# A ternary feed-forward kernel on one core: the second block, too, does layer 1 by seven products of halves

## The chip, the core and the metric

The kernel runs on one core of a Trainium2 chip. A core has five engines that work side by side, each through its own queue in order: TensorE (PE in the profile; its weight loads are PEld), VectorE (DVE), ScalarE (ACT), GpSimd (POOL) and SyncE (SP), which here only issues transfers. The metric is the time of one execution on the device in microseconds (us). For one execution there is also a trace of every instruction; its span is the time from the first instruction to the last.

## The reference

```python
w = weights[conditions]                          # one 64 x 64 matrix for each of 128 samples
c = jnp.einsum('bct,bcd->bdt', x, w)             # x: (128, 64, 512)
h = gelu(c @ ternary(W1).T + b1)                 # 512 -> 2048
y = h @ ternary(W2).T + b2                       # 2048 -> 512
# ternary(W) = alpha * sign(W) * (|W| > 0.05 * max|W|), alpha the mean of |W| where the mask holds
scale = jnp.max(jnp.abs(y)) / 7 + 1e-8           # over the whole of y
out = x + jnp.clip(jnp.round(y / scale), -7, 7) * scale
```

## The kernel before

The 128 samples make 8192 rows ("tokens") of 512 values. They are worked on in NB = 16 blocks of 512 tokens; a block is four pairs of samples. For each block the kernel does three things on TensorE: it mixes x by the samples' matrices (`mix`, into the PSUM tile `pc`), it does layer 1 (PSUM, then Gelu on ACT), and it does layer 2, which gathers in four PSUM tiles `py`. The 2048 hidden values are taken in NH = 16 steps of 128. Layer 2 runs LAG = 2 steps behind layer 1. The first is the exception: block 0 does all of its layer 1, then nearly all of its layer 2 (steps 0 to 13) in a loop of its own, in which ACT and DVE also finish preparing the weights.

To keep precision, every moving operand is held as two fp32r parts, hi and lo: ACT copies a tile to hi, DVE subtracts it to get lo (`split`), and each product is done with both. The ternary weights are kept as fp8 tiles `w1t` and `w2t`; before each use a step's weights are widened into fp32r (`widen1`, `widen2` on POOL; `widen7` on POOL and, for group 2, on DVE).

There are two forms of a block.

- An ordinary block (`eight`): each step is 8 matmuls of 512 columns for layer 1 and 8 for layer 2. Its x is conditioned by `condition`: four pairs j, for each a mix on PE, one ACT copy to hi and one DVE subtraction to lo, in a pair of large tiles `x`.
- A block in SEVEN (`pair`, `seven`): two steps at a time. Layer 1 of the two is a 2 x 2 product of halves, done with seven products in place of eight, each of 4 matmuls of 256 columns, into the PSUM tiles `xy` and `z`. It needs sums of quarters of x (`t1` to `t4`) and sums of quarters of the weights (`w1f[1]` to `w1f[3]`), and DVE and ACT put the products together in `ring`. Its x is conditioned by `condition7`: for each pair j a mix, three ACT copies out of `pc` (`b12`, the hi parts of `xb` and `xl`), four DVE sums over x in place, two DVE subtractions (lo of `xb` and `xl`), and then a part that is returned to the caller, one ACT copy of the four sums to hi (`xt`) and one DVE subtraction to lo. In `pair` that last part runs in the following pair of steps; in `eight` it runs at once:

```python
for part in condition7(n + 1, j, extra["x"][:, j % 2, :], two_next[-1]):
    part()
```

Everything is issued through `InOrder`, which pins an instruction behind all that was written before it for the same engine. So the text of the program is the order of each engine's queue. In the loop of block 0's layer 2 this order is, after the matmuls of step hc:

```python
if hc in (4, 6, 8, 9):        # g = 0, 1, 2, 3
    count2(g)                 # ACT: masks <- terns, with a sum
    kept(w2t, g, terns2)      # ACT: the fp8 weights of layer 2
if hc in (5, 7, 9, 11):       # j = 0, 1, 2, 3
    condition(1, j, pair_of(x_next, j), two_next)
    for g in {7: [0], 9: [1], 11: [2, 3]}.get(hc, []):
        sum2(g)               # DVE: nat <- nat, terns, with a sum
```

Ahead of these, at steps 0 and 3, DVE has `signed2(2)` and `signed2(3)` (`terns` from `nat` and `junk`), and at step 1 six subtractions `low`. `alpha_2` turns the sums of `count2` and `sum2` into the scale of layer 2 (a small matmul `total`, then four small DVE instructions); the first `result` (DVE: y out of `py`) needs it. PSUM holds two `pc` tiles at a time, two of `ph` (or `xy`) and four of `py`; in the blocks of SEVEN `z` takes one of the two places of `pc`.

SyncE's queue issues all loads of x and the stores. POOL's queue also gathers the samples' matrices (`fetch`) and puts them in place (`place`).

Of the kernel before, what the change touches and what calls it, by code (L numbers as in the profile page):

```python
# [19 lines left out]
P = 128  # L20
# [17 lines left out]
def tile_cond_ternary_ffn(  # L38
# [24 lines left out]
    GH = NH // NG  # L63
    WCH = GH * T
    LAG = 2
    SEVEN = range(2, 14)
    KNOWN = NB - 2
    AWAY = 2
    HALF = BLK // 2
# [172 lines left out]
    def flat(w):  # L242
        return w.rearrange("p a b -> p (a b)")
# [10 lines left out]
    def group1(tiles, g):  # L254
        return tiles[g // 2][:, g % 2, :]
# [118 lines left out]
    def widen2(n, hc):  # L374
        if n == 0 and hc < NH - LAG:
            w = w2f[hc % 4]
        elif n == NB - 1 and hc == NH - 1:

            w = flat(w1f[0])
        else:  # L380
            w = w2f[hc % 2]
        if n == 0 and hc < NH - LAG:
            g, i = divmod(hc, GH)
            pool.tensor_copy(w, group1(terns2, g)[:, i * T : (i + 1) * T])
        else:
            pool.tensor_copy(w, w2t[:, hc])
        wide2[n, hc] = w
# [28 lines left out]
    def low(n, hc):  # L416

        open_low.pop((n, hc), lambda: None)()
# [202 lines left out]
    w1t = big.tile([P, NH, T], F8, tag="big", name="w1t")  # L621
    x_next = load_x(1)

    def kept(t, g, tiles):

        act.copy(flat(t[:, g * GH : (g + 1) * GH]), group1(tiles, g), saturate=False)

    for hc in range(NH - LAG):
        if hc + 2 < NH - LAG:
            widen2(0, hc + 2)  # L630
        layer2(0, hc)
        if hc == 0:
            signed2(2)
        if hc == 1:
            for i in range(10, NH):
                low(0, i)
        if hc < NG:
            kept(w1t, hc, terns)
        if hc == 3:
            signed2(3)  # L640
        if hc == 4:
            two_next = parts(1)
            w2t = big.tile([P, NH, T], F8, tag="big", name="w2t")
        if hc in (4, 6, 8, 9):
            g = {4: 0, 6: 1, 8: 2, 9: 3}[hc]
            count2(g)
            kept(w2t, g, terns2)
        if hc in (5, 7, 9, 11):
            j = (hc - 5) // 2
            condition(1, j, pair_of(x_next, j), two_next)  # L650
            for g in {7: [0], 9: [1], 11: [2, 3]}.get(hc, []):
                sum2(g)
    cond[1] = two_next
    x_next, two_next, fetched = [], [], []
    hf = ring[:2]
    widen1(1, 0)
    widen2(0, NH - LAG)

    w1p = w1t.rearrange("p (k two) m -> p k two m", two=2)
    a11, a12 = w1p[:, :, 0, : 2 * P], w1p[:, :, 0, 2 * P :]
    a21, a22 = w1p[:, :, 1, : 2 * P], w1p[:, :, 1, 2 * P :]
# [51 lines left out]
    def quarter_x(n, j):  # L716

        sp.dma_start(out=extra["x"][:, j % 2, :], in_=x_blk[n][:, j, :])

    def product(out, w, b, first):  # L720
        for c in range(2):
# [149 lines left out]
    def eight(s):  # L871

        n, hc = steps[s]
        if s + 1 < len(steps):
            ahead = steps[s + 1]
            if ahead[0] not in SEVEN:
                widen1(*ahead)
            else:
                for g in (3, 0):
                    widen7(0, g)  # L880
        widen2(*steps[s + 1 - LAG])
        if n + 1 < NB:
            if hc == 0:
                if n + 1 == SEVEN[0]:
                    extra["x"] = half.tile([P, 2, T], F32, tag="half", name="x_quarters")
                    for j in range(2):
                        quarter_x(n + 1, j)
                else:
                    x_next.append(load_x(n + 1) if n + 1 < NB - 1 else split_x(n + 1))
                two_next.append(parts7(n + 1) if n + 1 in SEVEN else parts(n + 1))  # L890
            if 2 <= hc < 2 + PAIRS:
                fetched.append(fetch(n + 1, hc - 2))
            if 7 <= hc < 7 + PAIRS:
                place(hc - 7, fetched[hc - 7 - PAIRS])
        if n == KNOWN and hc in (0, 1):
            fetch_x(order[hc])
        two = half.tile([P, 2, BLK], F32R, tag="half", name=f"h_{n}_{hc}")
        two = [two[:, k, :] for k in range(2)]

        for part in halves if s == len(steps) - 1 else [slice(0, BLK)]:  # L900
            ph = ps_h.tile([P, BLK], F32, tag="ph", name=f"ph_{n}_{hc}_{part.start}")
            ph = ph[:, part]
            layer1(n, hc, ph, part)

            bend(n, hc, ph, [t[:, part] for t in two], ph if n == NB - 1 else hf[hc % 2])
        hidden[n, hc] = two
        if s + 1 < len(steps) and steps[s + 1][0] in SEVEN and n not in SEVEN:
            widen7(0, 1)
            widen7(0, 2)
        if n + 1 < NB and 8 <= hc < 8 + PAIRS:  # L910
            j = hc - 8
            if n + 1 in SEVEN:
                for part in condition7(n + 1, j, extra["x"][:, j % 2, :], two_next[-1]):
                    part()
                if j + 2 < PAIRS:
                    quarter_x(n + 1, j + 2)
            else:
                condition(n + 1, j, pair_of(x_next[-1], j), two_next[-1])
            cond[n + 1] = two_next[-1]
        if hc == LAG:  # L920
            for j in range(PAIRS):
                largest(n - 1, j)
            keep(n - 1)
        if n == KNOWN and hc == LAG:
            tops_known.append(widened(ymax[:, :KNOWN], "known"))
        if s == len(steps) - 1:
            return
        if s == NH + 1:
            alpha_2()
        layer2(*steps[s - LAG])  # L930
        if steps[s - LAG][1] == NH - 1:
            for j in range(PAIRS):
                result(n - 1, j)
        if n == KNOWN and hc == LAG + 1:
            largest_of(tops_known.pop(), top_known, ps_c, "pc")
            steps_of(scale, inverse, top_known)
        if n == KNOWN and hc > LAG + 1:
            advance(2 if hc in (6, 9, 12, 15) else 1)
        if n == NB - 1:
            advance(1)  # L940
# [15 lines left out]
    def pair(n, k, finish):  # L956

        s = n * NH + 2 * k
        ahead = (k + 1) % (NH // 2)
        leaves = ahead == 0 and n + 1 not in SEVEN  # L960
        before = steps[s - 2], steps[s - 1]

        def second(i):
            layer2(*before[i // PAIRS], [i % PAIRS])

        def results(js):
            for j in js:
                result(n - 1, j)

        def behind(i):  # L970
            if i == 0:
                finish()
                if k == 1:
                    results(range(2, PAIRS))
                widen2(*before[1])
                if k == 0:
                    two_next.append(parts7(n + 1) if n + 1 in SEVEN else parts(n + 1))
            if i == 1 and not leaves:
                widen7(ahead, 1)
            if i == 2:  # L980
                if parting:
                    parting[0][0]()
                if leaves:
                    widen1(n + 1, 0)
                else:
                    widen7(ahead, 0)
            if i == 4:
                if not leaves:
                    widen7(ahead, 3)
                if k < PAIRS:  # L990
                    fetched.append(fetch(n + 1, k))
                if 2 <= k < 2 + PAIRS:
                    place(k - 2, fetched[PAIRS * (n - 1) + k - 2])
                if not leaves:
                    widen7(ahead, 2)
                if parting:
                    parting.pop()[1]()
                if k == 1:
                    quarter_x(n + 1, 0)
                    quarter_x(n + 1, 1)  # L1000
                if k in (4, 5):
                    quarter_x(n + 1, k - 2)
                if 3 <= k < 3 + PAIRS:
                    xp = extra["x"][:, (k - 3) % 2, :]
                    if n + 1 in SEVEN:
                        parting.append(condition7(n + 1, k - 3, xp, two_next[-1]))
                    else:
                        condition(n + 1, k - 3, xp, two_next[-1])
                    cond[n + 1] = two_next[-1]
            if i == 5:  # L1010
                widen2(*steps[s])
            if i == 6 and k == 0:
                results([0])
            if i == 7:
                if k == 0:
                    results([1])
                if k in (1, 2):
                    for j in (2 * k - 2, 2 * k - 1):
                        largest(n - 1, j)
                if k == 2:  # L1020
                    keep(n - 1)

        return seven(n, k, behind, second)
# [131 lines left out]
```

## Time and profile before

| What | Value |
|---|---|
| Median of 3 runs | 999.9 us (999.79 to 1000.32) |
| The profiled execution | 999.93 us |
| Its span | 998.1 us |
| Mean granted TensorE clock in it | 0.996 |
| PE busy | 983.1 us (98%) |
| DVE, ACT, POOL busy | 693.1 (69%), 603.1 (60%), 577.0 us (58%) |
| Share of PE in the chain that ended last | 97% |

The page of the profile gives the busy time of each engine and the chain of work that ended last, followed back from the last instruction. The views in order of time list an engine's instructions, neighbours of one kind merged: start, length, engine, line, operation, output and inputs with their shapes, count, and in brackets the idle time before it and who ended it. Nearly all instructions bear line 34, that of the helper `InOrder`; they are told apart by their tiles. Numbers of tiles are left out: `wf` is `w1f` and `w2f`, `x` the tiles of `condition`, `h` the hidden parts, `nat`, `terns`, `masks` and `junk` those of the weights' preparation.

### The profile page before, as it was taken

Reading aid. Unit: us, or ns where it says so; the run is one execution under the profiler, and the core shown is the slowest. Engines: PE = TensorE matmul, PEld = TensorE weight load, DVE = VectorE, ACT = ScalarE, POOL = GpSimd, SP = SyncE. Lnnn points to the kernel's source line nnn. Section 1 sums busy time; section 2 is a strip of 40 time slices with the busy share of each in tenths; the row PEclk is TensorE's granted clock in tenths of the full one; section 3 lists DMA queues with packets and bytes.
Section 4 is the critical chain, followed back from the end, with each engine's and each line's share of the span. In section 5 each row is a group of like instructions: output and inputs, shape, how many; then the busy total and the mean of one; then the engine's idle time right before and its main releaser. Section 6 shows DMA issues by size and latency. Waiting matters only on the chain.

```text
span 998.1 us, 17056 instructions
## 1 busy us (share of the span) xinstructions
PE 983.1 (98%) x5865; PEld 869.1 (87%) x5866; DVE 693.1 (69%) x1316; ACT 603.1 (60%) x1078; POOL 577.0 (58%) x916
## 2 busy tenths in 40 slices
PE   8999999999999999999999999999999999999995
PEld 5887889999999998999999999999999989888884
DVE  7897347677677767677677676767667675567865
ACT  7994445656556565565655565565565655467663
POOL 6866446566564655656565564655656556465433
PEclk9999999999999999999999999999999999999998
DMA  9201011110111101011110011101011110349993
GB/s 360 85 22 45 15 32 49 32 56 20 28 47 34 57 23 68 14 32 48 34 56 24 24 47 41 50 23 66 14 33 48 33 58 23 128 157 367 384 408 121
DMA packets 33159, 80.06 MB, mean 80 GB/s; under 512 B 3760, under 2 KB 3760, under 8 KB 30128
## 3 DMA queue, kind: packets, MB, share of 16 engines
q1 hardware_dynamic: 31024, 76.86, 21.6%
q0 software_dynamic: 2048, 2.10, 0.7%
q8 instruction: 47, 0.77, 0.3%
q14 instruction: 40, 0.33, 0.1%
HBM read 46.44 MB, written 32.51 MB: 79 GB/s over the span
## 4 chain that ended last, share of the span: by engine, by line
PE 97%; DVE 2%; DMA 1%; ACT 0%; SPq 0%; issue 0%
PE py L34 46%; PE xy L34 18%; PE z L34 14%; PE ph L34 12%; PE pc L34 6%; DMA nat<-in_L_ffn_W 1%; DVE top L34 1%; DVE xt L34 0%; PE number L34 0%; DVE ymax L34 0%; DVE y_last L34 0%; SPq L34 0%; DVE x L34 0%; ACT x L34 0%; ACT ph L34 0%
## 5 line engine op out<-in xcount | busy, mean ns | idle before, releaser
L34 PE MATMUL py<-wf,h 128*128 128x512 f32 x2048 | 498.4, 394 | 0.0
L34 PEld LDWEIGHTS py<-wf,h 128*128 128x128 f32 x2048 | 376.5, 188 | 76.5 <-DVE y L34 1.6
L34 POOL CAST wf<-w2t 128x512 fp32r<-128x512 fp8e4 x242 | 167.1, 696 | 219.1 <-PE py L34 215.1
L34 DVE TENSOR_TENSOR ring<-xy,ring 128x256 f32<-128x256 f32 x192 | 107.0, 557 | 171.7 <-PE xy L34 169.1
L34 DVE TENSOR_TENSOR h<-ring,h 128x512 fp32r<-128x512 f32 x236 | 173.0, 757 | 73.9 <-ACT h L34 73.7
L34 ACT ACTIVATE ring<-ring,b1t,alpha_w 128x512 f32<-128x512 f32 x192 | 152.3, 817 | 84.3 <-DVE ring L34 84.3
L34 POOL CAST wf<-w1t 128x256 fp32r<-128x256 fp8e4 (+1 forms) x240 | 131.4, 550 | 69.9 <-PE xy L34 37.6
L34 ACT COPY ring<-xy 128x256 f32<-128x256 f32 x192 | 72.1, 375 | 150.9 <-PE xy L34 150.9
L34 POOL TENSOR_TENSOR wf<-w1t 128x256 fp32r<-128x256 fp8e4 x192 | 126.4, 658 | 51.8 <-PE xy L34 29.0
L34 ACT CAST h<-ring 128x512 fp32r<-128x512 f32 x240 | 142.3, 618 | 1.7
L34 PE MATMUL ph<-x,wf 128*128 128x512 f32 (+1 forms) x528 | 125.8, 384 | 0.3 <-DVE x L34 0.3
L34 PE MATMUL xy<-xt,wf 128*128 128x256 f32 x768 | 123.5, 283 | 0.0
L34 PE MATMUL xy<-xb,wf 128*128 128x256 f32 x768 | 122.7, 282 | 0.0
L34 PEld LDWEIGHTS xy<-xb,wf 128*128 128x128 f32 x768 | 111.7, 190 | 7.5
L34 PEld LDWEIGHTS ph<-x,wf 128*128 128x128 f32 x528 | 96.6, 188 | 20.1 <-DVE x L34 0.5
L34 PE MATMUL z<-xt,wf 128*128 128x256 f32 x768 | 107.8, 283 | 0.0
L34 PEld LDWEIGHTS xy<-xt,wf 128*128 128x128 f32 x768 | 106.0, 192 | 0.0
L34 PEld LDWEIGHTS z<-xt,wf 128*128 128x128 f32 x768 | 99.1, 192 | 0.0
L34 ACT COPY ring<-z 128x512 f32<-128x512 f32 x96 | 56.4, 587 | 56.4 <-PE z L34 56.4
L34 POOL COPY diag<-wg 64x64 f32<-64x64 f32 x128 | 48.7, 380 | 44.6 <-DMA wg<-in_L_cond_weights,rows 42.1
L34 ACT ACTIVATE ring<-ph,b1t,alpha_w 128x512 f32<-128x512 f32 x48 | 37.3, 778 | 57.4 <-PE ph L34 57.0
L34 POOL DMA_INDIRECT wg<-in_L_cond_weights,rows x64 | 64.0, 1000 | 11.6 <-issue 3.7
(111 smaller groups left out, 973.2 us busy)
## 6 DMA issues: line engine op xcount, KB each, us to landing
xt<-in_x SPq DMA_DIRECT2D x38, 512.0 KB, 7.5
y_dram<-y SPq DMA_DIRECT2D x15, 1024.0 KB, 3.9
out<-xt SPq DMA_DIRECT2D x30, 512.0 KB, 7.3
x_quarters<-in_x SPq DMA_DIRECT2D x52, 256.0 KB, 2.6
nat<-in_L_ffn_W SPq DMA_DIRECT2D x6, 1024.0 KB, 13.6
y_back<-y_dram SPq DMA_DIRECT2D x2, 1024.0 KB, 10.7
nat<-in_L_ffn_W SPq DMA_DIRECT2D x3, 512.0 KB, 9.6
wg<-in_L_cond_weights,rows POOLq DMA_INDIRECT x64, 2.7
```

The source lines that it names most:

```text
L34: return lambda *args, **kw: self._tc.keep_in_program_order(make(*args, **kw))
```

## The change

SEVEN begins with block 1 in place of block 2. Block 1's x is therefore conditioned by `condition7`, in the loop of block 0's layer 2, on x as it was loaded in one piece, with the last part run at once. At the end of that loop the first pair's weights are made by `widen7` for groups 3, 0, 1 and 2 in place of one `widen1`. The first block of `eight` after block 0 is now block 14, so `eight` loses its passage into SEVEN, and the quarters of x for block 2 are issued from `pair`. `alpha_2` moves from the second step of block 1 to a place behind the layer 2 of block 1's first pair. In the new text the functions of the seven products stand ahead of the loop, with nothing in them changed.

```diff
-    SEVEN = range(2, 14)
+    SEVEN = range(1, 14)
...
     for hc in range(NH - LAG):
...
         if hc == 4:
-            two_next = parts(1)
+            two_next = parts7(1)
             w2t = big.tile([P, NH, T], F8, tag="big", name="w2t")
...
         if hc in (5, 7, 9, 11):
             j = (hc - 5) // 2
-            condition(1, j, pair_of(x_next, j), two_next)
+            for part in condition7(1, j, pair_of(x_next, j), two_next):
+                part()
             for g in {7: [0], 9: [1], 11: [2, 3]}.get(hc, []):
                 sum2(g)
...
-    widen1(1, 0)
     widen2(0, NH - LAG)
+    for g in (3, 0, 1, 2):
+        widen7(0, g)
+    extra["x"] = half.tile([P, 2, T], F32, tag="half", name="x_quarters")
...
# in eight
-            if ahead[0] not in SEVEN:
-                widen1(*ahead)
-            else:
-                for g in (3, 0):
-                    widen7(0, g)
+            widen1(*ahead)
...
-                if n + 1 == SEVEN[0]:
-                    extra["x"] = half.tile([P, 2, T], F32, tag="half", name="x_quarters")
-                    for j in range(2):
-                        quarter_x(n + 1, j)
-                else:
-                    x_next.append(load_x(n + 1) if n + 1 < NB - 1 else split_x(n + 1))
-                two_next.append(parts7(n + 1) if n + 1 in SEVEN else parts(n + 1))
+                x_next.append(load_x(n + 1) if n + 1 < NB - 1 else split_x(n + 1))
+                two_next.append(parts(n + 1))
...
-        if s + 1 < len(steps) and steps[s + 1][0] in SEVEN and n not in SEVEN:
-            widen7(0, 1)
-            widen7(0, 2)
...
-        if s == NH + 1:
-            alpha_2()
         layer2(*steps[s - LAG])
...
# in pair, behind(i)
             if i == 6 and k == 0:
+                if n == 1:
+                    alpha_2()
                 results([0])
```

More of the change, by code (lines that the diff above doesn't have):

```diff
@@ L622, in tile_cond_ternary_ffn @@
     x_next = load_x(1)
[L624 to L641, printed above, removed]
-            two_next = parts(1)
[L643 to L649, printed above, removed]
-            condition(1, j, pair_of(x_next, j), two_next)
[L651 to L655, printed above, removed]
-    widen1(1, 0)
-    widen2(0, NH - LAG)
     w1p = w1t.rearrange("p (k two) m -> p k two m", two=2)
@@ L718, in quarter_x, with kept @@
         sp.dma_start(out=extra["x"][:, j % 2, :], in_=x_blk[n][:, j, :])
+    def kept(t, g, tiles):
+        act.copy(flat(t[:, g * GH : (g + 1) * GH]), group1(tiles, g), saturate=False)
+    for hc in range(NH - LAG):
+        if hc + 2 < NH - LAG:
+            widen2(0, hc + 2)
+        layer2(0, hc)
+        if hc == 0:
+            signed2(2)
+        if hc == 1:
+            for i in range(10, NH):
+                low(0, i)
+        if hc < NG:
+            kept(w1t, hc, terns)
+        if hc == 3:
+            signed2(3)
+        if hc == 4:
+            two_next = parts7(1)
+            w2t = big.tile([P, NH, T], F8, tag="big", name="w2t")
+        if hc in (4, 6, 8, 9):
+            g = {4: 0, 6: 1, 8: 2, 9: 3}[hc]
+            count2(g)
+            kept(w2t, g, terns2)
+        if hc in (5, 7, 9, 11):
+            j = (hc - 5) // 2
+            for part in condition7(1, j, pair_of(x_next, j), two_next):
+                part()
+            for g in {7: [0], 9: [1], 11: [2, 3]}.get(hc, []):
+                sum2(g)
+    cond[1] = two_next
+    x_next, two_next, fetched = [], [], []
+    hf = ring[:2]
+    widen2(0, NH - LAG)
+    for g in (3, 0, 1, 2):
+        widen7(0, g)
+    extra["x"] = half.tile([P, 2, T], F32, tag="half", name="x_quarters")
     def product(out, w, b, first):
@@ L906, in eight @@
         hidden[n, hc] = two
-        if s + 1 < len(steps) and steps[s + 1][0] in SEVEN and n not in SEVEN:
-            widen7(0, 1)
-            widen7(0, 2)
         if n + 1 < NB and 8 <= hc < 8 + PAIRS:
             j = hc - 8
[L912 to L918, printed above, removed]
+            condition(n + 1, j, pair_of(x_next[-1], j), two_next[-1])
             cond[n + 1] = two_next[-1]
```

## The prediction

> **What bounds the kernel now.** I read the page first (busy shares, then the chain that ended last), then PE in order of time, then ACT and DVE beside it in the stretch that the change rewrites.
>
> ```profile
> PE 983.1 (98%) x5865; PEld 869.1 (87%) x5866; DVE 693.1 (69%) x1316; ACT 603.1 (60%) x1078; POOL 577.0 (58%) x916
> ...
> PE 97%; DVE 2%; DMA 1%; ACT 0%; SPq 0%; issue 0%
> ```
>
> TensorE is busy 98% and carries 97% of the chain: a matmul column saved is time saved, as long as PE's operands are there. PE around block 1 (start, length, instruction):
>
> ```profile
> 82.60 1.98 PE L34 MATMUL ph<-x,wf 128*128 128x512 f32 x8
> ...
> 145.30 0.64 PE L34 MATMUL xy<-xb,wf 128*128 128x256 f32 x4
> ...
> 146.75 0.71 PE L34 MATMUL xy<-xt,wf 128*128 128x256 f32 x4
> ...
> 152.39 0.64 PE L34 MATMUL xy<-xb,wf 128*128 128x256 f32 x4
> ...
> 205.12 0.64 PE L34 MATMUL xy<-xb,wf 128*128 128x256 f32 x4
> ```
>
> Block 1 (ordinary) runs from 82.60 to 145.30, 62.70 us. Block 2 (seven products) from 145.30 to 205.12, 59.82 us; its first pair takes 7.09, the other seven 52.73. The third product of a pair, the first that needs w1f[2], starts 1.45 after the pair.
>
> Now ACT and then DVE during block 0's layer 2, where block 1's x is conditioned:
>
> ```profile
> 66.03 0.58 ACT L34 CAST x<-pc 128x512 fp32r<-128x512 f32 x1
> 66.51 1.91 ACT L34 ACTIVATE masks<-terns 128x2048 bf16<-128x2048 bf16 x1
> ...
> 68.41 1.89 ACT L34 CAST w2t<-terns 128x2048 fp8e4<-128x2048 bf16 x1
> ```
>
> ```profile
> 69.48 2.58 DVE L34 SCALAR_TENSOR_TENSOR terns<-nat,delta_w,junk 128x2048 bf16<-128x2048 f32 x1
> 71.98 1.27 DVE L34 TENSOR_TENSOR x<-pc,x 128x512 fp32r<-128x512 f32 x2
> 73.18 2.28 DVE L34 CUSTOM_DVE_ANT_0 nat<-nat,terns 128x2048 f32<-128x2048 f32 x1
> ...
> 78.69 0.69 DVE L34 TENSOR_TENSOR x<-pc,x 128x512 fp32r<-128x512 f32 x1 [3.22 <-ACT x L34]
> ```
>
> ACT runs without a gap here; a count2 and a kept together take 3.69 (66.51 to 70.20, where the next copy of x starts). DVE is 6 us behind: ACT has made hi of pair 0 at 66.03, DVE comes to its lo at 71.98. Today this doubles as slack, since each ACT copy needs only PE, and DVE follows at leisure. What the seven-product conditioning does when its last copy is not put off is seen in block 1, where block 2's x is made this way (ACT, then DVE):
>
> ```profile
> 116.02 0.26 ACT L34 COPY x_quarters<-pc 128x128 f32<-128x128 f32 x1
> ...
> 116.44 0.28 ACT L34 CAST xl<-pc 128x128 fp32r<-128x128 f32 x1
> 117.79 0.62 ACT L34 CAST xt<-x_quarters 128x512 fp32r<-128x512 f32 x1 [1.08 <-DVE x_quarters L34]
> ```
>
> ```profile
> 116.75 0.28 DVE L34 TENSOR_TENSOR x_quarters<-x_quarters,pc 128x128 f32<-128x128 f32 x1
> 116.95 0.81 DVE L34 TENSOR_TENSOR x_quarters<-pc,x_quarters 128x128 f32<-128x128 f32 x3
> ...
> 118.45 0.69 DVE L34 TENSOR_TENSOR xt<-x_quarters,xt 128x512 fp32r<-128x512 f32 x1 [0.16 <-ACT xt L34]
> ```
>
> ACT makes three copies (0.70 from the first start to the last end), then waits in its queue until DVE has made four sums (1.01), then copies hi; DVE's lo waits for that. It is a there-and-back between two queues, and the change puts it four times into the stretch where they are full.
>
> **The change part by part.** *Products.* A pair of ordinary steps has 16 layer-1 matmuls of 512 columns, 8 in 1.81 us by PE's rows, so 3.62. Seven products take 3.35 (152.39 to layer 2 at 155.74). Eight pairs: 2.2 us less. [...] Block against block the gain is 62.70 - 59.82 = 2.9, since block 1 also has a stop of 0.6 for y at 92 and the 0.14 of `total`.
>
> *The conditioning, walked through both queues.* DVE gets free for pair 0 at 71.98, as now: four sums to 72.99, then hi on ACT at 73.02. ACT, whose copies of pair 0 ended at 66.7, has stood 6.3 us, and everything behind hi in its queue (three count2 and kept, three pairs) is late. It goes on at 73.55, does count2(1) and kept(1) to 77.24, the copies of pair 1 to 77.94. DVE (lo of pair 0 done, 74.3) waits for these, 3.6 us; its sums end 78.98, hi(1) on ACT is 79.01 to 79.54 (to the next start), lo(1) ends 80.28, sum2(0) at 2.20 (79.30 to 81.50 in the trace) 82.48. ACT now has two count2 and two kept: 79.54 + 7.38 = 86.92; copies of pair 2 to 87.62; DVE has waited another 5.2. Sums to 88.66, hi(2) to 89.22, lo(2) to 89.96, sum2(1) to 92.16. ACT's copies of pair 3 are done at 89.92, but DVE's sums for it come after sum2(1): 92.16 to 93.17, its xb lo at 93.5, hi(3) to 93.8, lo(3) to 94.47. Then sum2(2) and sum2(3), 4.40: 98.87. Only then does DVE come to `widen7(0, 2)`, which now stands behind all this: first w1f[2] (0.42) at 99.29.
>
> *PE.* The 3rd mix needs pc of pair 0 back, 73.5, on time. The 4th needs that of pair 1 back, 79.5 instead of 78.07, so steps 12 and 13 end at 84.0 instead of 82.5. Then PE is out of work: product b11 needs xb of all pairs (93.5), the products with t1 and t4 need lo(3) (94.6), the one with t2 needs w1f[2] (99.32). That last wait ends latest: the pair stands as if begun at 99.32 - 1.45 = 97.87. Pair 1 follows at 104.96, block 2 at 104.96 + 52.73 = 157.69 against 145.30: **+12.4**, with the products' gain in it.
>
> *POOL and SP.* widen2(0, 14) waits for kept(3), now 86.9 instead of 78.1, and behind it stand widen7 of groups 3, 0 and 1 (0.64, 0.62, 0.64 + 0.40): done by 90, before 93.5, they cost nothing under that wait; without it 2.9 us of POOL work would stand against the 1.8 of step 13, about 1 us. The four gathers for block 2 (1.0 us each) move from steps 2 to 5 to pairs 0 to 3, the place that all later blocks use. The first two quarters of x, issued at 56.64, now go out in pair 1 and land in 2.6 us, needed in pair 3: nothing.
>
> *alpha_2.* Its matmul now stands behind the pair's layer 2, so DVE's first result of block 0 starts after it: 0.15 after pair 1's start plus 0.83 (90.33 to 91.16), where block 2 has it at 1.16 before (151.23). Two us late, and DVE has no idle time there: from 151.23 to 155.09 it goes straight into pair 1's additions. These come 2.1 late; gelu, casts and lo shift as far, and in pair 2 the copy of z must wait for the lo of hidden step 3, which reads the same ring tile: product t2 0.55 late, p5 1.06 late, and 0.25 for y in pair 1. With `total` 0.14: **+2.0**. Bounds: 0.14 if slack takes it, 2.2 if all of the delay lands.
>
> *The clock.* No stretch of the trace has PE idle for long; the record says 1.00 throughout. Its only cold stretch is the start, counted in 512-column matmuls:
>
> ```profile
> 3.00:7.00 4.00, 4.00 (x10) 1.38 (x10) 1.73 (x5) 0.88 (x1) 2.15 (x3) 1.00 0.96 395
> 7.00:15.00 8.00, 8.00 (x37) 3.55 (x36) 7.76 (x7) 7.49 (x5) 2.87 (x7) 1.00 1.03 393
> ```
>
> (PE's are the first count.) Ten in 4 us, then 37 in 8: 8.5 are missing at 0.216, 1.8 us. [...] Here PE is idle some 9 us, then 4 more ahead of t2. By the trace alone (1.00 throughout) the sum would have nothing[...]. I take **+1.8**, the cold row.
>
> Sum: 12.4 + 2.0 + 1.8 = 16.2 on the profiled execution's 999.93 us (span 998.1 and 1.8 around it), which stands 0.03 above the median of 999.9: **1016.1**.
>
> **The rivals.** *It works as meant.* If block 0's layer 2 covered the conditioning, block 1 would cost what block 2 does: 2.9 less, 997. For it: PE is the bound, and after 83 ACT is mostly idle. It decides in faster's favour only if w1f[2] is ready by 82.6 + 1.45 + 2.9 = 87.0; my walk misses that by 12, before alpha_2 and the clock. Against: DVE alone has 75.5 to 78.69 free, and gets 4 x 1.45 + 0.9 = 6.7 us more.
>
> *Only the work counts, not the order.* If ACT did not stand in hi (its later copies passing it), DVE would run on: today's end of sum2 at 87.31, plus 6.7, less the 3.2 idle: 90.8, so t2 at about 90.4 and pair 1 at 96.1. That is 8.9 less than the main case, near 1007. Against: 117.79 shows ACT standing for DVE with work behind it.
>
> *Worse.* The seven-product tiles take one more large buffer; if w2t got the one that `junk` leaves at 72.06, kept(0) would stand until then, the first sums come at 74.6 instead of 71.98, and all shifts by 2.6: 1018.7. [...]
>
> **How the numbers follow.** Main case 0.75, order free 0.10, worse 0.08, as meant 0.05, and 0.02 that the parts cancel to within 0.2% (2 us, about what a measurement of this kernel can tell from no change). Bounds of the main case: 16.2 - 1.8 - 1.86 = 12.5 to 16.2 + 1.6 + 0.2 = 18. I take 2 us below for some forty hand-overs added by hand, and above the buffer's 2.6: 1010.4 to 1020.4; left out are the order-free and the as-meant case. Faster 0.05, same 0.02, slower 0.93.
>
> **What would show it.** ACT waiting for DVE about 6.3 us ahead of its first `xt` cast at 73; DVE waiting for ACT 3.6 and 5.2 us before 88; a hole in PE from about 84 to 93.5 and one to 99.3 ended by DVE `wf`; a granted clock under 1.00 there; block 2's first `xy` near 161.5. I am wrong if PE's hole is under 5 us, if hi does not stand for DVE, or if something other than DVE's queue ends the hole.

## The result: 17 us slower, and the profile after

The changed kernel takes 1017.08 us (median; 1016.72 to 1018.11), the kernel before 1000.03 beside it: a ratio of 1.0173 (95% interval 1.0161 to 1.0184). Predicted were 1016.1, with a range of 1010.4 to 1020.4. The profiled execution took 1017.08 us, its span is 1015.3.

The busy shares and the chain that ended last, of the changed kernel:

```profile
PE 985.1 (97%) x5961; PEld 874.8 (86%) x5962; DVE 715.9 (71%) x1380; ACT 614.7 (61%) x1114; POOL 583.2 (57%) x932
...
PE 91%; DVE 5%; ACT 2%; issue 1%; DMA 1%; SPq 0%; ACTq 0%; DVEq 0%
```

PE has 96 more matmuls (8 pairs, 28 of 256 columns in place of 16 of 512). It has fewer columns and is busy 2.0 longer; part of its work ran at a lower clock, as seen below. DVE has 22.8 us more to do, ACT 11.6. The chain is the line to look at: PE carried 97% of it before and 91% now, and what it lost went to DVE and ACT. PE in order of time shows where (start, length, instruction, and in brackets the idle time before it and who ended it):

```profile
90.27 0.55 PE L34 MATMUL xy<-xb,wf 128*128 128x256 f32 x1 [5.46 <-ACT xb L34]
94.14 1.01 PE L34 MATMUL xy<-xb,wf 128*128 128x256 f32 x3 [3.33 <-DVE xb L34]
...
100.04 1.19 PE L34 MATMUL xy<-xt,wf 128*128 128x256 f32 x4 [2.99 <-DVE wf L34]
...
107.19 0.72 PE L34 MATMUL xy<-xb,wf 128*128 128x256 f32 x4
...
110.16 0.74 PE L34 MATMUL xy<-xt,wf 128*128 128x256 f32 x4 [1.31 <-ACT ring L34]
...
111.64 0.74 PE L34 MATMUL z<-xl,wf 128*128 128x256 f32 x4 [0.26 <-ACT ring L34]
...
116.35 0.64 PE L34 MATMUL xy<-xb,wf 128*128 128x256 f32 x4
...
162.07 0.64 PE L34 MATMUL xy<-xb,wf 128*128 128x256 f32 x4
```

PE has done block 0's layer 2 at 84.8 and then stands three times: for a hi and a lo of x, and for the weights w1f[2]. The second pair starts at 107.19 and takes 9.16 to the third at 116.35, where block 2's takes 7.01. From there block 1 runs as block 2 does: 45.72 for six pairs. Block 2 starts at 162.07 in place of 145.30, 16.77 later, nearly all of the 17.

Who stood for whom before that, ACT first and then DVE, in order of time:

```profile
73.39 0.63 ACT L34 CAST xt<-xt 128x512 fp32r<-128x512 f32 x1 [6.35 <-DVE xt L34]
```

```profile
78.34 0.29 DVE L34 TENSOR_TENSOR xt<-xt,pc 128x128 f32<-128x128 f32 x1 [3.60 <-ACT xl L34]
...
88.02 0.29 DVE L34 TENSOR_TENSOR xt<-xt,pc 128x128 f32<-128x128 f32 x1 [5.08 <-ACT xl L34]
...
99.48 0.42 DVE L34 TENSOR_TENSOR wf<-wf,w1t 128x256 fp32r<-128x256 f32 x1
```

ACT waits for DVE first, because hi needs DVE's sums; then DVE waits twice for ACT, which had been kept from its weights by the first wait. Neither engine was short of work in its queue. The last line is w1f[2], ready at 99.90: PE's third wait.

The stretches of PE's holes (span, then busy time and instructions of PE, PEld, DVE, ACT, POOL, then the granted clock, the DMA share and GB/s):

```profile
84.00:93.00 9.00, 1.36 (x5) 0.63 (x3) 4.79 (x11) 5.21 (x10) 5.49 (x6) 0.80 0.00 0
...
101.00:103.00 2.00, 2.00 (x12) 2.00 (x11) 0.42 (x1) 0.37 (x1) 0.81 (x2) 0.50 0.00 0
103.00:105.00 2.00, 2.00 (x12) 1.69 (x12) 1.83 (x4) 1.49 (x2) 1.24 (x2) 0.98 0.00 0
```

The granted clock is 0.50 from 89.43 to 103.08 (windows of half a microsecond give these ends). What PE does from 100.04 on, it does at half speed for 3 us: from one start to the next, four matmuls take 0.86 from 101.03, and 0.48 from 118.26.

### The profile page after: what moved, and what is told of

Its sections match the earlier page's. It is cut to its first block, busy times and chain, and to the rows that moved or that the text cites. A ratio compares the mean times of both kernels' runs of the same rounds, so it can differ in the third digit from the quotient of the medians.

```text
span 1015.3 us, 17395 instructions
## 1 busy us (share of the span) xinstructions
PE 985.1 (97%) x5961; PEld 874.8 (86%) x5962; DVE 715.9 (71%) x1380; ACT 614.7 (61%) x1114; POOL 583.2 (57%) x932
## 4 chain that ended last, share of the span: by engine, by line
PE 91%; DVE 5%; ACT 2%; issue 1%; DMA 1%; SPq 0%; ACTq 0%; DVEq 0%
PE py L34 43%; PE xy L34 20%; PE z L34 15%; PE ph L34 8%; PE pc L34 5%; DVE h L34 1%; DVE xt L34 1%; DMA nat<-in_L_ffn_W 1%; DVE nat L34 1%; DVE top L34 1%; ACT masks L34 1%; DVE junk L34 1%; ACT w2t L34 1%; DVE terns L34 1%; PE number L34 0%
## 5 line engine op out<-in xcount | busy, mean ns | idle before, releaser
L34 ACT ACTIVATE ring<-ring,b1t,alpha_w 128x512 f32<-128x512 f32 x208 | 165.1, 817 | 92.2 <-DVE ring L34 92.2
L34 POOL TENSOR_TENSOR wf<-w1t 128x256 fp32r<-128x256 fp8e4 x208 | 136.4, 656 | 66.1 <-PE xy L34 34.3
L34 PE MATMUL xy<-xb,wf 128*128 128x256 f32 x832 | 134.4, 284 | 8.8 <-ACT xb L34 5.5
L34 PE MATMUL xy<-xt,wf 128*128 128x256 f32 x832 | 134.5, 284 | 4.3 <-DVE wf L34 3.0
L34 PEld LDWEIGHTS xy<-xb,wf 128*128 128x128 f32 x832 | 121.7, 192 | 17.4 <-POOL wf L34 5.9
L34 PEld LDWEIGHTS xy<-xt,wf 128*128 128x128 f32 x832 | 115.4, 193 | 4.8 <-issue 3.3
L34 PE MATMUL z<-xt,wf 128*128 128x256 f32 x832 | 117.8, 284 | 0.0
L34 PE MATMUL ph<-x,wf 128*128 128x512 f32 (+1 forms) x400 | 94.2, 383 | 0.3 <-DVE x L34 0.3
L34 PEld LDWEIGHTS ph<-x,wf 128*128 128x128 f32 x400 | 72.6, 188 | 15.1 <-DVE x L34 0.5
L34 POOL DMA_INDIRECT wg<-in_L_cond_weights,rows x64 | 64.4, 1006 | 11.6 <-issue 3.6
L34 PE MATMUL z<-xl,wf 128*128 128x256 f32 x416 | 67.5, 285 | 0.3 <-ACT ring L34 0.3
```

Source lines behind the costliest of these rows:

```text
L34: return lambda *args, **kw: self._tc.keep_in_program_order(make(*args, **kw))
```

## The experiments

Each time is the median of its kernel; the kernel before, run beside them, stood at 1000.01 to 1000.04. All start from the changed kernel unless another is named.

**The order of hi.** Is it that ACT's copy to hi stands for DVE's sums with work queued behind it? The parts of the conditioning that come last (hi, lo) are put off by two steps or more for pairs 0 to 2:

```diff
-            for part in condition7(1, j, pair_of(x_next, j), two_next):
-                part()
+            if hc in (9, 11):
+                for _ in range(len(put_off) if hc == 9 else 1):
+                    for part in put_off.pop(0):
+                        part()
+            put_off.append(condition7(1, j, pair_of(x_next, j), two_next))
+            if hc == 11:
+                for part in put_off.pop(0):
+                    part()
```

> Only the place of the put-off part of the conditioning changes: ACT's copy of the four sums to hi and DVE's lo of pairs 0 and 1 come at step 9 behind the last kept, that of pair 2 at step 11 ahead of pair 3's copies. Same instructions, same count. Theory (ACT standing in hi for DVE, with count2 and kept behind it, is what stretches both queues): ACT has its last kept done at about 78.7 instead of 87.3, DVE its last lo at 87.1 and w1f[2] at 92.0; the product with t2 starts near 92 instead of 100.0, so about 8 us less, and up to 1.3 less again if the clock does not fall: 1007.5 to 1009. Rival (the added DVE work itself is what is too much, in whatever order): under 2 us gained, 1015 or more.

Measured: 1010.28 (1009.28 to 1010.72), ratio to before 1.0099 (1.0083 to 1.0114). PE in order of time:

```profile
86.00 0.38 PE L34 MATMUL xy<-xb,wf 128*128 128x256 f32 x1 [2.67 <-POOL wf L34]
...
92.89 1.20 PE L34 MATMUL xy<-xt,wf 128*128 128x256 f32 x4 [2.98 <-DVE wf L34]
```

With the same instructions in another order the product with w1f[2] comes at 92.89 in place of 100.04. That is 7.15, and 6.8 of it arrives in the time. The order is the largest cause, as the theory had it; the time lies 1.3 above its band. The clock fell here too (0.50 from 87.05 to 97.3), which the expectation had left open: 3.55 from this product to the layer 2. When it fell, only stops of 2.67 and 0.40 lay behind PE; the one of 2.98 came later.

**What stands ahead of w1f[2] on DVE.** The last two sums go behind `widen7`:

```diff
-            for g in {7: [0], 9: [1], 11: [2, 3]}.get(hc, []):
+            for g in {7: [0], 9: [1]}.get(hc, []):
                 sum2(g)
...
         widen7(0, g)
+    sum2(2)
+    sum2(3)
```

> Only DVE's order changes: the first pair's weights of group 2 come ahead of sum2 of groups 2 and 3 instead of behind them. Theory (the end of PE's hole is set by w1f[2] standing behind two sums of 2.2 us): the product with t2 follows the products with t1 and t4 at about 97 instead of 100.0, 3 us less, 1014.0; the two sums then delay the pair's additions and alpha_2, but these wait for PE anyway. Rival (the hole is set by the conditioning's lo, and the sums only change places with the additions): within 0.5 us of 1017.1, since what w1f[2] gains is given back at the results.

Measured: 1014.26 (1013.0 to 1014.95), ratio 1.014 (1.0125 to 1.0156). The same product starts at 96.73, with no wait, and the second pair at 103.98 in place of 107.19. The third of PE's waits was DVE's order alone, and it cost about 3.

**alpha_2.** It goes back ahead of the layer 2 of the pair:

```diff
# in pair, behind(i)
+                if n == 1 and k == 0:
+                    alpha_2()
...
-                if n == 1:
-                    alpha_2()
                 results([0])
```

> Only the place of alpha_2 changes: its matmul stands ahead of the layer 2 of block 1's first pair instead of behind it. Theory (the second pair's 9.16 us against 7.01 come from DVE's results starting 2 us late, behind alpha_2): the second pair takes about 7.0, the whole 2.0 to 2.2 less, 1015.0. Rival (the second pair is slow from the backlog of DVE out of block 0 or from the cold clock): within 0.3 us of 1017.1.

Measured: 1015.19 (1014.92 to 1015.86), ratio 1.0149 (1.0134 to 1.0165). PE in order of time:

```profile
108.11 0.64 PE L34 MATMUL xy<-xb,wf 128*128 128x256 f32 x4
...
115.12 0.64 PE L34 MATMUL xy<-xb,wf 128*128 128x256 f32 x4
```

The second pair takes 7.01 again, 2.15 less than in the changed kernel. In this execution the clock stayed low for 17.1 us (0.50 from 88.2 to 105.3) and the first pair's layer 2 lay partly in that spell: 4.47 in place of 3.66, which took back about 0.8.

**The clock.** PE's first hole is filled with 44 idle matmuls of tiles that lie there (128x512, bf16, 212 ns each), with no other edit:

```diff
+    warm = ps_h.tile([P, T], F32, tag="ph", name="warm")
+    for _ in range(44):
+        pe.matmul(out=warm, lhsT=ones_b, rhs=group2(3)[:, :T], start=True, stop=True)
```

> 44 matmuls of 512 bf16 columns into a PSUM tile that nobody reads are added behind step 13's layer 2, to fill PE's hole from 84.8 to about 94; everything else is as after the change. Theory (the clock fell to half from 89.4 to 103.05 because PE was idle, and this made the first pair's products 1.34 us longer): the granted clock stays 1.00, 1.3 to 1.4 less, 1015.7. Rival (the products were slow for another reason, operands for one, or the clock falls for another cause): the clock stays up and the time stays within 0.3 us of 1017.1. If the 44 take longer than the hole, some of the gain is given back.

Measured: 1017.51 (1016.73 to 1017.76), ratio 1.0172 (1.0158 to 1.0186): no gain, and neither theory's reason. The matmuls held the clock at 1.00 through the first hole. PE and the windows behind the second:

```profile
100.08 0.80 PE L34 MATMUL xy<-xt,wf 128*128 128x256 f32 x4 [3.76 <-DVE wf L34]
```

```profile
100.00:101.00 1.00, 0.92 (x6) 0.95 (x7) 0.39 (x1) 0.09 (x1) 0.92 (x2) 0.78 0.00 0
101.00:102.00 1.00, 1.00 (x7) 1.00 (x7) 0.16 (x1) 0.28 (x1) 0.43 (x2) 0.50 0.07 16
...
104.00:105.00 1.00, 1.00 (x6) 0.78 (x5) 0.93 (x3) 0.80 (x2) 0.85 (x2) 1.00 0.00 0
```

The second hole, 3.76 us, was enough by itself. The clock fell at about 100.6, half a microsecond after PE had begun to work again, and the work then ran at half speed for 3.4 us. So both holes are filled, the second by 16 more behind the first products of the pair:

```diff
+            if i == 1 and n == 1 and k == 0:
+                again = ps_c.tile([P, T], F32, tag="pc", name="warm_again")
+                for _ in range(16):
+                    pe.matmul(out=again, lhsT=ones_b, rhs=group2(3)[:, :T], start=True, stop=True)
```

> As the run that filled PE's first hole, with 16 further idle matmuls between the pair's products with t4 and t2, so that both holes are filled (3.4 of the 3.75 us of the second). There the clock held through the first hole and fell for 3.4 us just after the second. Theory (each hole[...] costs the clock, and the clock is worth 1.3 us here): the granted clock stays 1.00 through the pair, the products from t2 to layer 2 take 2.0 us instead of 3.3, and the time is 1.3 less than after the change, 1015.8. Rival (the clock is not what makes this pair slow, or filling matmuls cost as much as they save): within 0.4 us of 1017.1.

Measured: 1015.47 (1015.28 to 1017.16), ratio 1.0157 (1.0143 to 1.0171), 1.6 below the changed kernel's median, though the two intervals overlap. The place itself is plainer. In PE's order:

```profile
100.26 0.71 PE L34 MATMUL xy<-xt,wf 128*128 128x256 f32 x4 [0.29 <-DVE wf L34]
...
102.25 3.82 PE L34 MATMUL py<-wf,h 128*128 128x512 f32 x16
```

The clock is 1.00 in every window from 93 to 109, and the product with w1f[2] is 1.99 ahead of the layer 2, as in block 2; in the changed kernel it was 3.33. The clock costs 1.34.

**All of the order at once.** The last parts of the conditioning go where DVE has had time, `widen7` stands ahead of the sums, `kept(3)` stands last, the sums of groups 0 and 1 go behind the loop, and those of groups 2 and 3 wait for the first pair:

```diff
-        if hc in (4, 6, 8, 9):
+        if hc in (4, 6, 8):
...
+        if hc == 8:
+            put_off.pop(0)()
+            put_off.pop(0)()
         if hc in (5, 7, 9, 11):
-            for part in condition7(1, j, pair_of(x_next, j), two_next):
-                part()
-            for g in {7: [0], 9: [1], 11: [2, 3]}.get(hc, []):
-                sum2(g)
+            hi, lo = condition7(1, j, pair_of(x_next, j), two_next)
+            put_off.append(lambda hi=hi, lo=lo: (hi(), lo()))
+        if hc == 9:
+            count2(3)
+        if hc == 10:
+            for g in (3, 0, 1, 2):
+                widen7(0, g)
+            put_off.pop(0)()
+        if hc == 11:
+            put_off.pop(0)()
+            kept(w2t, 3, terns2)
...
-    for g in (3, 0, 1, 2):
-        widen7(0, g)
+    sum2(0)
+    sum2(1)
...
# in pair, behind(4), n == 1 and k == 0
+                    sum2(2)
+                    sum2(3)
```

> The same instructions as after the change in another order. ACT: count2 and kept of groups 0 to 2, then hi of pairs 0 and 1, pair 2's copies, count2(3), hi of pair 2, pair 3's copies and hi, and kept(3) last. DVE: the first pair's weights of group 2 ahead of lo of pair 2, and no sum2 in the loop: groups 0 and 1 behind it, 2 and 3 behind the first pair's additions. Theory (order made the hole): lo of pair 3 is done at 82.3 and PE finds its operands at 82.9, no hole and no fall of the clock. What is left is DVE's amount of work: its sums end near 93.4, alpha_2 is 3.5 us late for the second pair's layer 2, and with the delay this hands to the third pair the time is 1001 to 1003. Rival (order cannot cure it, DVE and ACT have too much to do ahead of block 1): a hole of over 5 us stays, 1006 or more.

Measured: 1004.88 (1004.84 to 1005.45), ratio 1.0049 (1.0035 to 1.0063): 12.2 less than the changed kernel, 1.9 above the expected band, and still slower than before. PE:

```profile
82.80 0.64 PE L34 MATMUL xy<-xb,wf 128*128 128x256 f32 x4
...
94.78 0.36 PE L34 MATMUL total<-sums,ones_f 128*128 128x8 f32 x2 [4.82 <-DVE sums L34]
```

The first pair starts at 82.80 with no hole ahead of it, so the order made the holes. But the wait has moved. `total`, the matmul of alpha_2, stands in PE's own queue ahead of the second pair's products; it needs DVE's last sum, which ends at 94.6. That the first of those products would have had their operands is seen where two sums are left out, below: there they start at 90.05. The clock fell at the end of this hole too (0.50 from 95.0 to 98.4).

**Can DVE be relieved?** From the reordered kernel, three more. First the lo of pairs 0 to 2 goes to POOL, all of them issued at step 11, behind `widen7` in POOL's queue:

```diff
-        return lambda: act.copy(hi, t8), lambda: dve.tensor_tensor(lo, t8, hi, ALU.subtract)
+        engine = pool if n == 1 and j < 3 else dve
+        return lambda: act.copy(hi, t8), lambda: engine.tensor_tensor(lo, t8, hi, ALU.subtract)
...
```

> As the reordered kernel, with the lo of pairs 0 to 2 on POOL instead of DVE (three subtractions of 0.61 less for DVE, about 1.3 to 1.6 each on POOL, which is free from 76). Theory (after the reordering DVE's amount of work up to alpha_2 is what costs): 1.8 us less than the reordered kernel, 999.5 to 1001. Rival (POOL and DVE slow each other, or POOL's widening for the next steps is now late): no gain or a loss against it.

Measured: 1005.74 (1005.19 to 1006.01), ratio 1.0055 (1.0041 to 1.0068). A miss: three subtractions fewer, and the sums begin no sooner. DVE:

```profile
80.41 0.29 DVE L34 TENSOR_TENSOR xt<-xt,pc 128x128 f32<-128x128 f32 x1 [1.32 <-ACT xl L34]
```

This wait and one of 1.43 at 76.72 hold the time that was freed. DVE now waits for ACT's copies, and the last sum still ends at 94.9. PE also stayed at half speed for longer in this execution than in the reordered kernel's: the pair's second product with `xb` (four matmuls) took 1.05 here, from 99.35, and 0.64 there, from 98.66. That is part of the 0.9 that it lost against that.

Then two of the four sums are left out, which tells what they cost:

```diff
+    pool.memset(sums2, 0.0)
...
# in pair, behind(4), n == 1 and k == 0
-                    sum2(2)
-                    sum2(3)
```

> As the reordered kernel, with sum2 of groups 2 and 3 left out (the scale of layer 2 then has half of its sum): 4.4 us less for DVE ahead of alpha_2. Theory (order and then DVE's work up to alpha_2 are all that stands between this change and its gain): the second pair takes about 7.1 and block 1 as long as block 2, 59.8 to 60, which is 2.7 to 2.9 less than before the change: 997.1 to 997.6. Rival (the seven products of block 1 cost something else at their place): 999 or more.

Measured: 1002.23 (1001.17 to 1003.99), ratio 1.002 (1.0013 to 1.0027). Also a miss. `total` waits for nothing now (89.91), but PE shows a new wait:

```profile
94.35 0.74 PE L34 MATMUL xy<-xt,wf 128*128 128x256 f32 x4 [2.64 <-ACT ring L34]
...
100.53 0.64 PE L34 MATMUL xy<-xb,wf 128*128 128x256 f32 x4
```

The second pair, begun at 90.05, takes 10.48. DVE is late twice in it: its additions for the first pair stand behind sum2(1) and begin at 87.3, and the results of block 0 begin only behind the late alpha_2, ahead of the next additions. The 21 times form two groups, and the trace is one of the first: nine of 1001.17 to 1001.55 at a mean clock of 0.996, twelve of 1002.15 to 1003.99 at 0.993 to 0.995. A spell of 3.4 us at half speed, as long as the one measured with the first hole filled, takes 0.0017 off that mean (half of 3.4 in a span of 999.5), so I estimate that the clock fell in the twelve and not in the nine; no trace shows one of the twelve.

The end of that line: no sums of layer 2's weights at all, and alpha_2 ahead of the layer 2 of the first pair.

```diff
-    sum2(0)
-    sum2(1)
...
# in pair, behind(i)
+                if n == 1 and k == 0:
+                    alpha_2()
...
-                if n == 1:
-                    alpha_2()
```

> As the reordered kernel, with all four sum2 left out (the scale of layer 2 is then nought) and alpha_2 ahead of the first pair's layer 2: DVE has 9 us less to do ahead of the results, and these start as in block 2. Theory (order, the place of alpha_2 and DVE's work up to the results are all that stands between the change and its 2.9 us): block 1 takes 59.8 plus 0.14 for the total, block 2 starts near 142.8, 997.3. Rival (something else in block 1, the widening on POOL or the way x is laid out, keeps it slow): 999 or more.

Measured: 997.65 (997.53 to 997.86), ratio 0.9976 (0.9966 to 0.9985). PE:

```profile
82.82 0.64 PE L34 MATMUL xy<-xb,wf 128*128 128x256 f32 x4
...
142.78 0.64 PE L34 MATMUL xy<-xb,wf 128*128 128x256 f32 x4
```

Block 1 takes 59.96, block 2's 59.82 and `total`'s 0.14. The gain by the seven products is there, 2.4 in the time, and what stands between the reordered kernel and it is four DVE instructions of 2.2 us each together with the later place of alpha_2, which needs them.

Last, everything is computed, and the work is spread over the engines with room. From the reordered kernel: the lo of block 0's hidden steps 12 to 15 and of pairs 0 to 2 on POOL, group 3's sum by ACT in two halves (`above2`), sum2(0) at step 7, sum2(1) at 10, sum2(2) behind the loop, and alpha_2 ahead of the pair's layer 2:

```diff
-            open_low[n, hc] = lambda: dve.tensor_tensor(two[1], hf, two[0], ALU.subtract)
+            late = pool if hc >= 12 else dve
+            open_low[n, hc] = lambda: late.tensor_tensor(two[1], hf, two[0], ALU.subtract)
...
-        return lambda: act.copy(hi, t8), lambda: dve.tensor_tensor(lo, t8, hi, ALU.subtract)
+        engine = pool if n == 1 and j < 3 else dve
+        return lambda: act.copy(hi, t8), lambda: engine.tensor_tensor(lo, t8, hi, ALU.subtract)
...
+    def above2(i):
+        act.activation(
+            group1(masks, 2 + i), flat(nat2[3]), AF.Relu, bias=delta[1],
+            scale=[1.0, -1.0][i], accum_out=relu2[:, i : i + 1],
+        )
...
```

> An attempt at the whole result with less on DVE: as the reordered kernel, with lo of pairs 0 to 2 and the last four low of block 0 on POOL (idle from 76 to 84), the sum of group 3 by two Relu sums on ACT plus delta times the count in place of sum2(3), sum2(0) and sum2(1) in the gaps of the conditioning, and alpha_2 inside the first pair's layer 2. Theory (DVE's work up to the results costs): 6 us less of it there, results at most 0.5 late, 997.5 to 999, less than before the change. Rival (POOL's subtractions of 1.3 us slow DVE[...], or ACT's Relu sums delay the first pair's copies): 1000 or more.

Measured: 1004.96 (1004.8 to 1005.35), ratio 1.005 (1.0037 to 1.0064). The rival's reason. PE, then DVE, then POOL:

```profile
84.84 3.35 PE L34 MATMUL py<-wf,h 128*128 128x512 f32 x7 [3.62 <-POOL h L34]
```

```profile
80.28 3.37 DVE L34 CUSTOM_DVE_ANT_0 nat<-nat,terns 128x2048 f32<-128x2048 f32 x1
```

```profile
77.36 1.29 POOL L34 TENSOR_TENSOR h<-ring,h 128x512 fp32r<-128x512 f32 x1
78.59 2.92 POOL L34 TENSOR_TENSOR xt<-xt,xt 128x512 fp32r<-128x512 f32 x2
81.46 3.32 POOL L34 TENSOR_TENSOR h<-ring,h 128x512 fp32r<-128x512 f32 x1
```

DVE's sum takes 3.37 in place of 2.28, POOL's subtraction 3.32 in place of 1.29. Look at the ends. DVE's sum ends at 83.65, which is 2.28 behind 81.37, about where POOL's two subtractions of x end (81.51). POOL's next, begun at 81.46, ends at 84.78, which is 1.29 behind 83.49, about the end of DVE's sum. So, as the ends have it, each stood until the other was done. The kernel before shows longer times side by side too: its last two sums take 2.65 and 2.69 in place of 2.28, and POOL's casts beside them 2.33 and 2.67 in place of 0.61.

PE then waits 3.62 in layer 2 for POOL's late hidden part and goes on at half speed: the seven matmuls from 84.84 take 3.15, 0.45 each (0.23 in the next layer 2, 16 in 3.66 from 100.84), and four of 256 columns take 0.85 from 87.99 and 0.48 only from 91.19 on. The second pair starts at 97.35, against 90.05 with no sums: of these 7.3, the wait is 3.6, and the matmuls from 84.84 to the end of the first pair's layer 1 take some 2.8 longer than at full clock. The subtractions that went from DVE to POOL did not relieve DVE while its own sums ran: the two sums beside them took 3.37 and 3.36 (from 80.28 and 86.50) in place of 2.28.

No version that computes everything was faster than the kernel before. Not tried: `total` behind the second pair's products in the reordered kernel.

## Why the prediction was right

Its sum was the right one, and so were the sizes but two, whose errors partly cancel: the clock was put 0.46 too high, alpha_2 0.29 too low. A wait for w1f[2] that ended 0.72 later than forecast makes up the rest.

- *ACT and DVE waiting in turn.* Predicted 6.3 for ACT, then 3.6 and 5.2 for DVE; measured 6.35, 3.60 and 5.08. Shown as the cause by the order of hi (6.8 less) and by the reordered kernel (no hole at all).
- *w1f[2] ends the hole.* Predicted done at 99.29, the product at 99.32; it was done at 99.90, the product at 100.04. 0.3 of the 0.7 is that block 0's layer 2 began that much later in this execution, 0.2 one sum that took 2.48, the rest hand-overs.
- *The clock, over-sized.* Predicted 1.8, from the 8.5 matmuls that are missing at the start; measured 1.34 (3.33 against 1.99). Of the spell of 13.65 only the work that lay in it was charged: the 3 us from 100.04 on, while the layer 2 (103.37) began with the clock back. That the clock would fall in PE's holes was my estimate, and so was the 1.6 for it in the upper bound. That the trace says 1.00 throughout was misread: it does so while PE works, but after PE's last product (986.2; one small matmul follows at 989.57) the clock falls to 0.50 at 990.4, so the kernel before already showed the fall.
- *alpha_2, slightly under.* Predicted 1.86 and 0.14 for `total`; measured 2.15 (9.16 against 7.01) and 0.14, together 0.1 over the upper bound of 2.2: all the delay of DVE's first result landed. Shown by moving it: 7.01 again. The split was wrong: PE waits 1.31 ahead of the product with t2 and 0.26 ahead of the fifth product (`z` from `xl`), where 0.55 and 1.06 were forecast, because already ACT's copy of `xy` stood for DVE's lo of the hidden part, 3.60. For y PE lost 0.03 in place of 0.25.
- *POOL and SP at nothing.* POOL waited 12.30 for `w2t`, to 87.51, and its `widen7` was done by 90.7, ahead of the operand that PE awaited to 94.14. Without that cover I had put about 1 us on it; with hi put off PE did wait for POOL, 2.67.
- *The sum.* 12.4 predicted to block 2, 0.72 later for w1f[2], 2.15, 0.14, 1.34 and 0.03 in a layer 2: 16.8, against 16.77 in the trace.

*The rivals.* "Only the work counts" was put near 1007, and the reordered kernel's 1004.88 says what that rival had right: the order is worth some 12 here, more than the 8.9 I gave it. With w1f[2] ahead of the sums, the product with t2 starts at 84.23 there, where the rival had 90.4, and part of that is lost again at `total`. "As meant" was put at 997; that is 997.65 once the sums are gone and alpha_2 stands early. So both describe versions of the kernel, but not this one. Left open is how the last 7 split in the reordered kernel between DVE's amount of work and the place of `total`: leaving two sums out took 2.65 away, and the last step took the other two sums and moved alpha_2 together.

## What to carry to other kernels

When a step is moved into a stretch where two in-order queues are full, walk both queues instruction by instruction: a copy that needs the other engine's sum holds back all behind it, and the other engine then waits for that (here 6.35, then 3.60 and 5.08). A wait that is taken away shows the next one, here hi, w1f[2], then the sums that alpha_2 needs; the gain in PE's columns comes only when the last is gone. Before work goes from one engine to another, look in the trace for what the two cost each other side by side (here 3.37 in place of 2.28 and 3.32 in place of 1.29).

## What the runs showed of the hardware

The granted clock fell 3.6 to 5.3 us after PE had begun its stop: 4.6 in the changed kernel, 5.3 with the weights first, 3.6 with alpha_2 early, 4.2 with the first hole filled, 5.0 in the reordered one. With the first hole filled and in the reordered kernel PE was at work again by then, for 0.5 and 0.2 us, and so it was with hi put off, where stops of 2.67 and 0.40 were enough. In the traced execution with both holes filled it did not fall (1.00 in every window from 85 to 94 and from 93 to 109). The low spells lasted 3.4 us with the first hole filled and in the reordered kernel, 10.2 with hi put off and with the weights first, 13.65 in the changed kernel and 17.1 with alpha_2 early: one, three, four and five times 3.41. What I had not expected is that the short hole was no cheaper than the long ones. In the changed kernel, with some 9 and 3 us, the clock cost 1.34. With the first hole filled, 3.76 us cost 1.5: 3.16 to the layer 2 in place of 1.99, and 4.14 from there to the next pair in place of 3.82.

With the work spread, DVE's sum and POOL's subtractions ran beside each other, and by their ends the later of the two waited for the rest of the other (3.37 in place of 2.28, 3.32 in place of 1.29). The busy shares count that wait as work: the trace has each as one instruction of that length.
